# First loads in smaller pieces behind a warm-up product, and two pieces of VectorE work moved off the round changes, in a two-layer mixing and feed-forward kernel

## The chip, the core and the metric

The kernel runs on one core of one Trainium2 chip, in float32. The metric is the device time of one execution in microseconds, as the median of several runs. One execution is also taken by the hardware profiler; all instruction times below come from that one.

## The reference, cut to what matters

The input x has 32 samples of 128 channels by 2048 columns. The first layer computes `x + F(M(x))`. M mixes the 128 channels of each sample with a kernel of its own, a sum of eight matrices weighted by a softmax of the sample's condition. F multiplies the 2048 columns by a 2048 x 2048 matrix W and adds a low-rank update:

```
out = jnp.einsum('bsd,od->bso', x, W) + bias
xa  = jnp.einsum('bsd,erd->ebsr', x, A)
w   = coeffs * scales
upd = jnp.einsum('ebsr,eor,e->bso', xa, Bf, w)
return out + upd
```

The second layer is a grouped convolution with nine taps along the columns, then sixteen heads of a feed-forward block (128 to 512 to 128, with a Gelu) over permuted columns.

## The kernel before, in words

Mixing by channel and multiplying by columns commute, so the kernel first multiplies x by the whole weight and mixes afterwards.

**The weight.** W plus the low-rank update (256 ranks, in two halves c of 128) is made in 16 blocks of 512 x 2048 numbers. `w_make` (L150) makes one: four times two products of a piece of A with a piece of B^T (L156), and a VectorE add of W to each result (L160). It stores the block with a DMA on GpSimd's queue (L162). The ranks have factors `wsc`, coeffs times scales; before, they are multiplied into B^T by `low_scale` on VectorE (L140). A and B^T are loaded in four quarters of 512 columns each by `load_low`, each half c by a DMA of its own, all on SP's queue. Four blocks are made before the first step. The rest are made two to a step in the first round.

**The big product.** It is done by Strassen-like recursion: seven outer products P1, P2, P6, P7, P5, P3, P4, called rounds, each with eight steps g (four samples each), 56 steps in all. A step (`multiply`, L256) is itself seven inner products of 4 x 2 TensorE records (L272), 24.03 us in all. Their results lie in three PSUM banks: P1, P6, P7, P4 go to px, P2 to pz, P5 and P3 to py. In time they run P1 (px), P2 (pz), P6 (px), P5 (py), P7 (px), P3 (py), P4 (px). VectorE adds each result to SBUF (L265) before the next product into the same bank may start; in the first round ScalarE copies those that are new (L267). `inner_weights` (L175) makes three or four differences of weight blocks once per round: on VectorE before the first step, on GpSimd later, during step g=7 of a round or just before it (L179 to L185, about 4.5 us each). `x_combine` (L213) makes the four sums of x for a step on GpSimd, `outer_weights` (L303) combines weight blocks for the coming round there.

**Order.** The order of every engine's instructions is the order of the Python program (a manual schedule); each queue runs in that order. Between the inner products, `between(j)` hands small pieces of other work to the engines. One piece is `mixed_kernel` (L337): eight VectorE instructions on 128 x 128 numbers (L345, L347) that make the mixed kernel of one sample, two after each of the first four products. Kernel b = (round - 1) * 7 + g falls to step g of each round after the first, for g = 0 to 6, until 32 are made; after 16 of them GpSimd stores the buffer (L349). The generator `small` (L578) is advanced once at the end of each step: the condition's layers, products of the weight's column sums with ones (L672), then the matrices of the convolution (tw): three loads at the end of step 6 (L680 to L682), four VectorE instructions (L684 to L687) and a store on SP's queue (L688) at the end of step 7, the last of round P1.

**Buffers.** A pool of 24 SBUF buffers of 8 KB per partition holds nearly everything; a load waits on SP's queue until its buffer is free. From the last round on, the mixing, convolution and feed-forward work (L381, L436, L540, L551) are interleaved with it and follow it.

Of the kernel before, what the change touches and what calls it, by code (L numbers as in the profile page):

```python
# [11 lines left out]
ALU = mybir.AluOpType  # L12
# [4 lines left out]
P = 128  # L17
B = 32
L = 2048
QW = 512  # L20
KEXP = 8
# [4 lines left out]
NQ = QW // 2  # L26
# [4 lines left out]
NG = B // GB  # L31
# [11 lines left out]
def adaln_ffn_kernel(  # L43
# [16 lines left out]
    A: bass.AP,  # L60
    BfT: bass.AP,
    coeffs: bass.AP,
    scales: bass.AP,
    toep: bass.AP,
    cwT: bass.AP,
    ffw: bass.AP,
# [3 lines left out]
    nc = tc.nc  # L70
# [8 lines left out]
    def slot(name, shape=(P, L)):  # L79
        return big.tile(list(shape), FP, name=name, tag="s")  # L80


    def bank():
        return banks.pop(0)

    def done(*ps):
        banks.extend(ps)
# [29 lines left out]
    wsc = const.tile([P, 2], FP, name="wsc", tag="wsc")  # L117
    cs = const.tile([P, 4], FP, name="cs", tag="cs")


    nc.sync.dma_start(cs[:, 0:2], coeffs)
    nc.sync.dma_start(cs[:, 2:4], scales)
    nc.vector.tensor_tensor(wsc, cs[:, 0:2], cs[:, 2:4], ALU.mult)
    a_sb = [slot(f"a_sb{c}") for c in range(2)]
    bf_sb = [slot(f"bf_sb{c}") for c in range(2)]

    def load_low(k, o):

        for c in range(2):
            if o is not None:  # L130
                cols = bass.ts(o, QW)
                nc.sync.dma_start(bf_sb[c][:, cols], BfT[c, :, cols])
        for c in range(2):
            if k is not None:
                nc.sync.dma_start(a_sb[c][:, bass.ts(k, QW)], A[c, :, bass.ts(k, QW)])

    def low_scale(o):
        for c in range(2):
            cols = bf_sb[c][:, bass.ts(o, QW)]
            nc.vector.tensor_scalar(cols, cols, wsc[:, c : c + 1], None, ALU.mult)  # L140

    wsum = slot("wsum", (P, NPH, QW))
    seen = set()

    def w_load(kh, oh, ki, oi):
        t = slot(f"w_{kh}{oh}{ki}{oi}", (P, 4, QW))
        nc.sync.dma_start(t.rearrange("p k o -> p (k o)"), WT[kh, oh, ki, oi])
        return t

    def w_make(t, kh, oh, ki, oi):  # L150
        o = 2 * oh + oi
        for kc in range(4):
            pw = bank()
            i0 = kh * 1024 + ki * 512 + kc * P
            for c in range(2):
                nc.tensor.matmul(  # L156
                    pw, lhsT=a_sb[c][:, i0 : i0 + P], rhs=bf_sb[c][:, bass.ts(o, QW)],
                    start=(c == 0), stop=(c == 1),
                )
            nc.vector.tensor_tensor(t[:, kc], pw, t[:, kc], ALU.add)  # L160
            done(pw)
        nc.gpsimd.dma_start(wb_d[kh, oh, ki, oi], t.rearrange("p k o -> p (k o)"))  # L162

    def row_sums(t, oh, oi):
        o = 2 * oh + oi
        ks = t.rearrange("p k o -> p o k")
        if o in seen:
            part = agp.tile([P, QW], FP, name=f"part_{len(seen)}", tag="sn", bufs=2)
            nc.vector.tensor_reduce(part, ks, AX.X, ALU.add)
            nc.vector.tensor_tensor(wsum[:, o], wsum[:, o], part, ALU.add)  # L170
        else:
            nc.vector.tensor_reduce(wsum[:, o], ks, AX.X, ALU.add)
        seen.add(o)
# [15 lines left out]
    def x_load(g, tp, kh):  # L189
        t = slot(f"xt_{g}{tp}{kh}", (P, 2, 2, QW))  # L190
        nc.sync.dma_start(t.rearrange("p k s c -> p (k s c)"), xT[g, tp, kh])
        return t
# [385 lines left out]
    def small():  # L578
# [3 lines left out]
        def load(name, src, rows, cols, eng=nc.scalar):  # L582
            t = sm[0:rows, used[0] : used[0] + cols]
            used[0] += cols
            if src is not None:
                eng.dma_start(t, src)
            return t
# [17 lines left out]
        ones = load("ones", None, P, P)  # L605
# [63 lines left out]
        wbc = slot("wbc", (P, NPH, QW))  # L669
        for o in range(NPH):  # L670
            p5 = bank()
            nc.tensor.matmul(p5, lhsT=ones, rhs=wsum[:, o], start=True, stop=True)  # L672
            nc.scalar.copy(wbc[:, o], p5)
            done(p5)
        nc.sync.dma_start(w1_d, wbc.rearrange("p f n -> p (f n)"))
# [5 lines left out]
        nc.sync.dma_start(tw[:, 2], toep[:, 0])  # L681
        nc.sync.dma_start(tw[:, 3], toep[:, 2])  # L682
        yield
        nc.vector.tensor_tensor(tw[:, 1], tw[:, 2], tw[:, 3], ALU.add)  # L684
        nc.vector.tensor_scalar(tw[:, 1], tw[:, 1], 0.5, None, ALU.mult)  # L685
        nc.vector.scalar_tensor_tensor(tw[:, 0], t1, 0.5, tw[:, 1], ALU.mult, ALU.add)  # L686
        nc.vector.scalar_tensor_tensor(tw[:, 1], t1, -0.5, tw[:, 1], ALU.mult, ALU.add)  # L687
        nc.sync.dma_start(tw_d, tw.rearrange("p k r c -> p (k r c)"))  # L688
        yield
# [6 lines left out]
        for kh, oh in ((0, 0), (0, 1), (1, 1), (1, 0)) for ki in range(2) for oi in range(2)  # L696
    ]
    first = {}
    load_low(0, 0)
    wt = {k: w_load(*k) for k in blocks[0:1]}  # L700
    low_scale(0)
    load_low(None, 1)
    low_scale(1)
    wt[blocks[1]] = w_load(*blocks[1])
    load_low(1, None)
    xs = {0: [x_load(0, 0, 0)]}
    for k in blocks[2:4]:
        wt[k] = w_load(*k)

    def make(k):  # L710
        t = wt.pop(k)
        w_make(t, *k)
        made.append(k)
        if len(made) > 4:
            row_sums(t, k[1], k[3])
        return t

    steps = [(r, g) for r in ROUNDS for g in range(NG)]
    xs[0] += [x_load(0, 1, 0), x_load(0, 1, 1)]
    load_low(2, 2)  # L720
    load_low(3, 3)
    lhs = {}
    for n, k in enumerate(blocks[0:4]):
        first[k[2:]] = make(k)
        if n == 1:
            lhs[0] = x_combine(*steps[0], xs.pop(0))
    low_scale(2)
    low_scale(3)
    rhs = inner_weights("P1", first, nc.vector)
    unsummed = [(0, 0), (1, 0), (1, 1)]  # L730
    olds = {}
# [1 line left out]
    nxt, waiting, ts = {}, {}, {}  # L733
# [8 lines left out]
    for i, (r, g) in enumerate(steps):  # L742
        ri = i // NG
        last_round = ri + 1 == len(ROUNDS)
        if i + 1 < len(steps):
            if i + 1 not in xs:
                xs[i + 1] = x_loads(*steps[i + 1])
            if not last_round:
                lhs[i + 1] = x_combine(*steps[i + 1], xs.pop(i + 1))
                x_outer()  # L750
        if i + 2 < len(steps) and ri > 0 and not last_round:
            xs[i + 2] = x_loads(*steps[i + 2])
        if i == 0:
            olds_load(0)
        if i + 1 < len(steps) and not last_round:
            olds_load(i + 1)
        if g == NG - 1 and 0 < ri < len(ROUNDS) - 1:
            nxt = inner_weights(ROUNDS[ri + 1], nxt)

        if ri == 0:  # L760
            for k in blocks[4 + 2 * g : 6 + 2 * g]:
                t = make(k)
                if "late" in first:
                    b12 = first.pop("late")
                    row_sums(b12, 0, 1)
                    nc.vector.tensor_tensor(b12, first[1, 1], b12, ALU.subtract)
                if k[:2] == (1, 0):
                    nxt[k[2:]] = t
        elif ri + 1 < len(ROUNDS):
            for k, combine in waiting.items():  # L770
                nxt[k] = combine()
            waiting = {}
            if 2 <= g < 6:
                k = ((g - 2) // 2, (g - 2) % 2)
                waiting[k] = outer_weights(ROUNDS[ri + 1], *k)

        if last_round and g == 0:
            late_loads()
        k0 = 3 * (g - NG)
        if last_round:  # L780
            stage(k0, stage_first)

        def between(j):
            b = (ri - 1) * (NG - 1) + g
            if ri > 0 and g < NG - 1 and b < B and j < KEXP // 2:
                mixed_kernel(b, (2 * j, 2 * j + 1))
            if ri == 0 and j == 2:
                for k in blocks[6 + 2 * g : 8 + 2 * g]:
                    wt[k] = w_load(*k)
            if ri == 0 and j == 4 and unsummed:  # L790
                ki, oi = unsummed.pop(0)
                row_sums(first[ki, oi], 0, oi)
            if last_round:
                if j == 3 and i + 1 < len(steps):
                    lhs[i + 1] = x_combine(*steps[i + 1], xs.pop(i + 1))
                    olds_load(i + 1)
                if j in (2, 4):
                    stage(k0 + j // 2, stage_first)
                stage(k0 + j // 2, stage_third if j % 2 else stage_second)

        multiply(r, g, lhs.pop(i), rhs, olds.pop(i), between)
        next(chain, None)
        if last_round and g >= 6:
            pair(g - 6)
        if last_round and g == 7:
            gather_two(0)
        if g == NG - 1 and ri + 1 < len(ROUNDS):
            rhs = nxt if ri > 0 else inner_weights(ROUNDS[ri + 1], nxt)
            nxt = {}

    before = None
    for k, (g, h) in enumerate(heads):
# [5 lines left out]
        t = ts.pop(k)  # L818
# [70 lines left out]
```

## Time and profile before

| | |
|---|---|
| median of 3 runs | 2712.27 us (2712.09 to 2712.54) |
| profiled execution, its own time | 2712.6 us |
| its span, first to last instruction | 2710.8 us |
| TensorE busy | 2680.0 us in 6232 records |
| VectorE, GpSimd, ScalarE busy | 1266.6, 1087.6, 438.0 us |
| mean granted TensorE clock | 0.997 |
| first product (L156) starts | 7.35 us |
| first step's first product (L272) starts | 52.73 us |
| DMA moved | 608.03 MB, mean 224 GB/s |

How to read it: a float32 product of 128 x 128 by 128 x 512 shows as two records, each with a weight load before it. A line of a timeline or of a group gives the engine, the line of the program, the operation, what is written and read, shapes and a count; square brackets give the idle time before it and what ended it. The waits name the engine and the line that was waited for. A line can be that of a helper, so that all products of `multiply` have L272. Start and duration of a TensorE row are modelled, since its records overlap.

### The profile page before, as it was taken

The numbers are of one execution on the slowest core, as the hardware profiler recorded it, in microseconds if no ns is written. First come the engines' busy times: TensorE is split into PE (matmuls) and PEld (weight loads), VectorE is DVE, ScalarE is ACT, GpSimd is POOL, SyncE is SP. The second block draws the span as 40 slices with busy tenths as digits, with TensorE's granted clock in tenths as the row PEclk, the third lists the DMA queues.
The fourth block names the chain that finished last, engine by engine and source line by source line (L and its number), as shares of the span: only waits on it lengthen the run. The fifth ranks groups of instructions, "written<-read, shape, count | busy, mean of one in ns | idle before, by whom it ended". The sixth has DMA issues, their size and how long they took to land.

```text
span 2710.8 us, 18770 instructions
## 1 busy us (share of the span) xinstructions
PE 2680.0 (99%) x6232; PEld 1183.9 (44%) x6232; DVE 1266.6 (47%) x1934; ACT 438.0 (16%) x811; POOL 1087.6 (40%) x633
## 2 busy tenths in 40 slices
PE   8999999999999999999999999999999999999998
PEld 3444344444444444444444444444444444444443
DVE  5554333433445456432265555555555545555400
ACT  0000000000000000000000133333333333333332
POOL 3544546523655323647222233333334333333322
PEclk9999999999999999999999999999999999999999
DMA  8875547445465466575657888777777677777532
GB/s 339 344 295 224 205 192 306 152 186 205 158 258 233 176 240 253 215 285 195 216 191 234 260 286 247 228 233 230 212 222 231 214 219 231 227 226 239 168 116 85
DMA packets 184256, 608.03 MB, mean 224 GB/s; under 512 B 18016, under 2 KB 87904, under 8 KB 139744
## 3 DMA queue, kind: packets, MB, share of 16 engines
q1 hardware_dynamic: 148384, 465.36, 49.0%
q0 software_dynamic: 34144, 140.53, 15.1%
q10 hardware_dynamic: 1632, 0.96, 0.1%
q8 instruction: 50, 0.82, 0.1%
q14 instruction: 46, 0.38, 0.0%
HBM read 363.50 MB, written 209.72 MB: 211 GB/s over the span
## 4 chain that ended last, share of the span: by engine, by line
PE 96%; DVE 3%; issue 0%; DMA 0%; SPq 0%; POOLq 0%; DVEq 0%
PE bank L272 47%; PE bank L540 16%; PE bank L551 16%; PE bank L436 8%; PE bank L156 4%; PE bank L381 4%; DVE ags L347 2%; DVE u L265 0%; DVE tw L686 0%; DVE tw L685 0%; DMA a_sb<-in_A 0%; PE bank L672 0%; DVE p L265 0%; DMA out<-t,orow 0%; POOLq L884 0%
## 5 line engine op out<-in xcount | busy, mean ns | idle before, releaser
L540 PE MATMUL bank<-t,ws 128*128 128x512 f32 x1024 | 460.2, 592 | 0.0
L551 PE MATMUL bank<-gl,ws 128*128 128x512 f32 x1024 | 460.2, 592 | 0.0
L557 POOL DMA_INDIRECT out<-t,orow x128 | 154.9, 1210 | 662.7 <-DVE t L555 401.7
L543 ACT ACTIVATE gl<-bank 128x512 f32<-128x512 f32 x512 | 303.6, 597 | 689.1 <-PE bank L540 590.0
L272 PE MATMUL bank<-P_t,s_P 128*128 128x512 f32 x896 | 396.1, 595 | 6.2 <-DVE p L265 6.2
L265 DVE TENSOR_TENSOR u<-bank,u 128x512 f32<-128x512 f32 x280 | 187.8, 687 | 428.7 <-PE bank L272 419.6
L555 DVE TENSOR_TENSOR t<-bank,t 128x512 f32<-128x512 f32 x128 | 88.4, 691 | 557.8 <-PE bank L551 557.8
L540 PEld LDWEIGHTS bank<-t,ws 128*128 128x128 f32 x1024 | 194.6, 190 | 244.9 <-issue 241.3
L551 PEld LDWEIGHTS bank<-gl,ws 128*128 128x128 f32 x1024 | 194.6, 190 | 244.9 <-issue 236.8
L272 PE MATMUL bank<-wo_P,s_P 128*128 128x512 f32 x640 | 283.6, 593 | 3.3 <-DVE u L265 3.0
L272 PEld LDWEIGHTS bank<-P_t,s_P 128*128 128x128 f32 x896 | 170.9, 191 | 222.1 <-issue 221.4
L448 ACT ACTIVATE sn<-bank,ctxb 128x256 f32<-128x256 f32 x128 | 53.7, 471 | 1130.3 <-PE bank L436 1129.0
L436 PE MATMUL bank<-v,tw_l 128*128 128x512 f32 x512 | 235.6, 592 | 0.0
L371 POOL TENSOR_TENSOR x<-x,fb 128x2048 f32<-128x2048 f32 x32 | 144.7, 4522 | 168.7 <-DVE x L368 108.2
L272 PEld LDWEIGHTS bank<-wo_P,s_P 128*128 128x128 f32 x640 | 120.9, 190 | 159.0 <-issue 148.5
L265 DVE TENSOR_TENSOR p<-bank,p 128x512 f32<-128x512 f32 x112 | 77.3, 691 | 239.9 <-PE bank L272 239.7
L347 DVE SCALAR_TENSOR_TENSOR ags<-mix,att_bc,ags 128x128 f32<-128x128 f32 x224 | 185.9, 830 | 4.5
L272 PE MATMUL bank<-wo_P,xt 128*128 128x512 f32 x384 | 169.2, 592 | 0.0
L223 POOL TENSOR_TENSOR s_P<-xt 128x512 f32<-128x512 f32 x40 | 51.0, 1276 | 271.4 <-DMA xt<-in_xT 218.3
L523 POOL DMA_INDIRECT t<-hx_d,row x128 | 137.8, 1077 | 37.1 <-issue 33.6
L436 PEld LDWEIGHTS bank<-v,tw_l 128*128 128x128 f32 x512 | 97.2, 190 | 122.8 <-issue 121.5
L272 PE MATMUL bank<-P_t,xt 128*128 128x512 f32 x320 | 145.6, 598 | 3.1 <-DVE p L265 3.1
(114 smaller groups left out, 2493.5 us busy)
## 6 DMA issues: line engine op xcount, KB each, us to landing
xt<-in_xT SPq DMA_DIRECT2D x64, 1024.0 KB, 8.6
u<-u_d SPq DMA_DIRECT2D x40, 1024.0 KB, 10.6
wo_P<-wb_d SPq DMA_DIRECT2D x36, 1024.0 KB, 12.5
u<-c_d SPq DMA_DIRECT2D x64, 512.0 KB, 6.9
x<-in_x SPq DMA_DIRECT2D x32, 1024.0 KB, 8.8
xg<-x SPq DMA_DIRECT2D x256, 128.0 KB, 7.4
hx_d<-x1t SPq DMA_DIRECT2D x32, 1024.0 KB, 4.9
hx_d<-ht SPq DMA_DIRECT2D x32, 1024.0 KB, 7.3
```

The costliest lines, as they stand in the source:

```text
L156: nc.tensor.matmul(pw, lhsT=a_sb[c][:, i0 : i0 + P], rhs=bf_sb[c][:, bass.ts(o, QW)], start=(c == 0), stop=(c == 1),)
L265: nc.vector.tensor_tensor(to, ps, to, ALU.add)
L272: nc.tensor.matmul(ps, lhsT=lhs[k][:, bass.ts(kc, P)], rhs=rhs[k][:, kc], start=first and kc == 0, stop=last and kc == 3, skip_group_check ...
L347: nc.vector.scalar_tensor_tensor(ag, mix[:, k], att, ag, ALU.mult, ALU.add)
L371: nc.gpsimd.tensor_tensor(xt, xt, late["fb"], ALU.add)
L381: nc.tensor.matmul(pm, lhsT=ag, rhs=u[:, f], start=True, stop=True)
L436: nc.tensor.matmul(ps, lhsT=late["tw"][:, k, r], rhs=v[k], start=first, stop=last, skip_group_check=True,)
L523: nc.gpsimd.indirect_dma_start(out=t.rearrange("p k t -> p (k t)"), out_offset=None, in_=hx_d[g].rearrange("l k t -> l (k t)"), in_offset= ...
L540: nc.tensor.matmul(pu, lhsT=w[:, m * P : (m + 1) * P], rhs=t[:, 0], start=True, stop=True)
L543: nc.scalar.activation(gl[:, m], pu, AF.Gelu)
L551: nc.tensor.matmul(pd, lhsT=w[:, (MC + m) * P : (MC + m + 1) * P], rhs=gl[:, m], start=(m == 0), stop=(m == MC - 1),)
L557: nc.gpsimd.indirect_dma_start(out=out, out_offset=bass.IndirectOffsetOnAxis(ap=orow[:, g, h : h + 1], axis=0), in_=t[:, 1], in_offset=None,)
```

## The change

It has five parts.

1. *First loads.* A and B^T are kept as two tiles of 1024 columns that hold both rank halves; the host lays them out so that one DMA brings both halves. The two small vectors come in one DMA. The first load of A is 128 columns, the first two of B^T 256 columns each; then come the remaining 384 of A's first quarter, and quarters.
2. *Scaling.* The factors are multiplied into A, not into B^T: A's quarters are scaled after their loads, the second quarter after the first block is made, the third and fourth after the fourth block.
3. *Warm-up.* TensorE first does two products of a zeroed tile that nothing reads. The first product of the first block is done in two halves of 256 columns.
4. *Conv matrices.* L684 to L687 are spread: the generator waits one step more, then L684 and L685 run at the end of step 8 (P2, g=0), L686 after step 9 and L687 with the store after step 10.
5. *Mixed kernels.* Kernel b = (round - 1) * 6 + g falls to g = 0 to 5; the last two are made in the last round, P4, at g = 0 and 1. The products with ones (L672) are done in two halves of 256 columns.

```diff
-    nc.sync.dma_start(cs[:, 0:2], coeffs)
-    nc.sync.dma_start(cs[:, 2:4], scales)
-    nc.vector.tensor_tensor(wsc, cs[:, 0:2], cs[:, 2:4], ALU.mult)
-    a_sb = [slot(f"a_sb{c}") for c in range(2)]
-    bf_sb = [slot(f"bf_sb{c}") for c in range(2)]
-    def load_low(k, o):
-        for c in range(2):
-            if o is not None:
-                cols = bass.ts(o, QW)
-                nc.sync.dma_start(bf_sb[c][:, cols], BfT[c, :, cols])
-        for c in range(2):
-            if k is not None:
-                nc.sync.dma_start(a_sb[c][:, bass.ts(k, QW)], A[c, :, bass.ts(k, QW)])
-    def low_scale(o):
-        for c in range(2):
-            cols = bf_sb[c][:, bass.ts(o, QW)]
+    a_sb = [slot(f"a_sb{h}", (P, 2, L // 2)) for h in range(2)]
+    bf_sb = [slot(f"bf_sb{h}", (P, 2, L // 2)) for h in range(2)]
+    def low(ts, c, i0, n):
+        h, i0 = divmod(i0, L // 2)
+        return ts[h][:, c, i0 : i0 + n]
+    def low_load(ts, src, i0, n):
+        h, j0 = divmod(i0, L // 2)
+        nc.sync.dma_start(ts[h][:, :, j0 : j0 + n], src[:, :, i0 : i0 + n])
+    def a_scale(i0, n):
+        for c in range(2):
+            cols = low(a_sb, c, i0, n)
             nc.vector.tensor_scalar(cols, cols, wsc[:, c : c + 1], None, ALU.mult)
+    def warm_up():
+        t = slot("warm", (P, QW))
+        nc.vector.memset(t, 0.0)
+        pw = bank()
+        for _ in range(2):
+            nc.tensor.matmul(pw, lhsT=t[:, 0:P], rhs=t, start=True, stop=True)
+        done(pw)
...
-            for c in range(2):
-                nc.tensor.matmul(
-                    pw, lhsT=a_sb[c][:, i0 : i0 + P], rhs=bf_sb[c][:, bass.ts(o, QW)],
-                    start=(c == 0), stop=(c == 1),
-                )
+            n = QW // 2 if i0 == 0 and o == 0 else QW
+            for o0 in range(0, QW, n):
+                for c in range(2):
+                    nc.tensor.matmul(
+                        pw[:, o0 : o0 + n], lhsT=low(a_sb, c, i0, P),
+                        rhs=low(bf_sb, c, o * QW + o0, n), start=(c == 0), stop=(c == 1),
+                    )
...
-            nc.tensor.matmul(p5, lhsT=ones, rhs=wsum[:, o], start=True, stop=True)
+            for half in (slice(0, NQ), slice(NQ, QW)):
+                nc.tensor.matmul(
+                    p5[:, half], lhsT=ones, rhs=wsum[:, o, half], start=True, stop=True
+                )
...
         yield
+        yield
         nc.vector.tensor_tensor(tw[:, 1], tw[:, 2], tw[:, 3], ALU.add)
         nc.vector.tensor_scalar(tw[:, 1], tw[:, 1], 0.5, None, ALU.mult)
+        yield
         nc.vector.scalar_tensor_tensor(tw[:, 0], t1, 0.5, tw[:, 1], ALU.mult, ALU.add)
+        yield
         nc.vector.scalar_tensor_tensor(tw[:, 1], t1, -0.5, tw[:, 1], ALU.mult, ALU.add)
         nc.sync.dma_start(tw_d, tw.rearrange("p k r c -> p (k r c)"))
...
-    load_low(0, 0)
+    warm_up()
+    nc.sync.dma_start(cs, coeffs)
+    low_load(a_sb, A, 0, P)
+    low_load(bf_sb, BfT, 0, QW // 2)
+    low_load(bf_sb, BfT, QW // 2, QW // 2)
+    nc.vector.tensor_tensor(wsc, cs[:, 0:2], cs[:, 2:4], ALU.mult)
+    a_scale(0, P)
+    low_load(a_sb, A, P, QW - P)
+    a_scale(P, QW - P)
     wt = {k: w_load(*k) for k in blocks[0:1]}
-    low_scale(0)
-    load_low(None, 1)
-    low_scale(1)
+    low_load(bf_sb, BfT, QW, QW)
     wt[blocks[1]] = w_load(*blocks[1])
-    load_low(1, None)
+    low_load(a_sb, A, QW, QW)
...
-    load_low(2, 2)
-    load_low(3, 3)
+    for i0 in (1024, 1536):
+        low_load(bf_sb, BfT, i0, QW)
+        low_load(a_sb, A, i0, QW)
     lhs = {}
     for n, k in enumerate(blocks[0:4]):
         first[k[2:]] = make(k)
+        if n == 0:
+            a_scale(QW, QW)
         if n == 1:
             lhs[0] = x_combine(*steps[0], xs.pop(0))
-    low_scale(2)
-    low_scale(3)
+    for i0 in (1024, 1536):
+        a_scale(i0, QW)
     rhs = inner_weights("P1", first, nc.vector)
...
-            b = (ri - 1) * (NG - 1) + g
-            if ri > 0 and g < NG - 1 and b < B and j < KEXP // 2:
+            b = (ri - 1) * (NG - 2) + g
+            if ri > 0 and g < NG - 2 and b < B and j < KEXP // 2:
                 mixed_kernel(b, (2 * j, 2 * j + 1))
```

## The prediction

> **What bounds the kernel now.** I read the page first, then TensorE's waits, then the timelines of the few places where TensorE stands still. The page says that TensorE is the bound: 2680.0 us of the span of 2710.8.
>
> ```profile
> PE 2680.0 (99%) x6232; PEld 1183.9 (44%) x6232; DVE 1266.6 (47%) x1934; ACT 438.0 (16%) x811; POOL 1087.6 (40%) x633
> ...
> PE 96%; DVE 3%; issue 0%; DMA 0%; SPq 0%; POOLq 0%; DVEq 0%
> ```
>
> The change takes no product away, so it can only gain what TensorE waits, and what it loses by running slowly. All its waits over the whole span:
>
> ```profile
> PE bank L272 <- DVE p L265: 9.7, 3, 6.2
> PE bank L156 <- DMA a_sb<-in_A: 7.4, 1, 7.4
> PE bank L272 <- DVE u L265: 3.0, 7, 0.5
> PE bank L156 <- DVE bf_sb L140: 1.2, 1, 1.2
> ```
>
> They sum to 21.3 us (columns: total, times, longest). Window by window: 7.4 and 1.2 lie in the first 40 us, 6.24 and 3.12 in the second round (P2), 0.3 in the third, 2.1 in the fourth, 0.8 in the sixth. After about 1173 us there is none.
>
> The longest, at the change from round P1 to P2, in the timelines of TensorE, VectorE and GpSimd (start, duration, instruction):
>
> ```profile
> 332.88 9.13 PE L272 MATMUL bank<-P_t,s_P 128*128 128x512 f32 x16 [6.24 <-DVE p L265]
> ...
> 317.71 4.62 DVE L685 TENSOR_SCALAR tw<-tw 128x512 f32<-128x512 f32 x1
> 322.36 4.88 DVE L686 SCALAR_TENSOR_TENSOR tw<-t,tw 128x512 f32<-128x512 f32 x1
> 327.27 4.87 DVE L687 SCALAR_TENSOR_TENSOR tw<-t,tw 128x512 f32<-128x512 f32 x1
> 332.06 0.68 DVE L265 TENSOR_TENSOR p<-bank,p 128x512 f32<-128x512 f32 x1
> ...
> 317.19 4.85 POOL L180 TENSOR_TENSOR P_t<-w,P_t 128x2048 f32<-128x2048 f32 x1
> 322.00 4.69 POOL L184 TENSOR_TENSOR w<-w,w 128x2048 f32<-128x2048 f32 x1
> 326.65 4.94 POOL L185 TENSOR_TENSOR P_t<-w,P_t 128x2048 f32<-128x2048 f32 x1
> ```
>
> The conv matrices (tw) run on VectorE step by step with the round's weight differences on GpSimd; the add that frees px is queued behind them. After the wait 16 records take 9.13 us, where 16 elsewhere take 7.03: another 2.10 us.
>
> The second place is step g=6 of round P2, where two mixed-kernel instructions meet two weight differences:
>
> ```profile
> 486.87 8.68 DVE L347 SCALAR_TENSOR_TENSOR ags<-mix,att_bc,ags 128x128 f32<-128x128 f32 x2
> ...
> 496.20 5.40 PE L272 MATMUL bank<-P_t,xt 128*128 128x512 f32 x8 [3.12 <-DVE p L265]
> ```
>
> 8 records take 5.40 instead of 3.60: 1.80 us more. Last the start:
>
> ```profile
> 7.35 30.36 PE L156 MATMUL bank<-bf_sb,a_sb 128*128 128x512 f32 x64 [7.35 <-DMA a_sb<-in_A]
> 38.89 14.00 PE L156 MATMUL bank<-bf_sb,a_sb 128*128 128x512 f32 x32 [1.18 <-DVE bf_sb L140]
> ...
> 40.27 0.49 DVE L140 TENSOR_SCALAR bf_sb<-bf_sb,wsc 128x512 f32<-128x512 f32 x1 [0.62 <-DMA bf_sb<-in_BfT]
> 40.67 2.28 DVE L179 TENSOR_TENSOR P_t<-w,w 128x2048 f32<-128x2048 f32 x1
> ...
> 47.53 2.48 DVE L160 TENSOR_TENSOR w<-bank,w 128x512 f32<-128x512 f32 x4
> ```
>
> A record costs 0.4292 us where TensorE runs freely (24.03 us for 56). 64 would take 27.5; they took 30.2 (30.36 less the 0.16 by which a record overlaps the next), so the slow beginning costs 2.7. And the DMA engines are full here:
>
> ```profile
> 15.00:45.00 30.00, 28.82 (x67) 12.46 (x66) 15.57 (x20) 0.00 (x0) 7.47 (x8) 1.00 1.02 414
> ```
>
> (the last two columns: DMA share 1.02, 414 GB/s).
>
> **What the Trainium skill says.** "SBUF — State Buffer", section "SBUF: two separate sides": VectorE and GpSimd share a port pair that one of them holds for a whole instruction. The trace agrees: L347 has a median of 0.352 us and a maximum of 4.637, beside GpSimd operations of 4.5. "TensorE: Matmul & The Clock Gate", "What's actually happening": the array runs at half clock until it has been busy for a window of about 3.4 us, and falls back after an idle one. Half speed agrees (weight loads 0.85 us apart until 12 us, 0.43 after); but here a wait of only 3.12 cooled it, and one of 1.18 did not (14.00 us for 32 records, 13.98 for the same 32 later). "DMA: Bandwidth & Descriptors", "Queues, rings and completion order": an engine takes turns between its queues. From 28 to 34 us loads moved 1.43 MB and GpSimd's stores 1.05 MB, which agrees.
>
> **The change part by part.**
>
> *Conv matrices.* The three blocked instructions leave the round change; L684 and L685 run at the end of step g=0 of P2, L686 at the end of g=1 and L687 at the end of g=2. Removed: 6.24 + 2.10 = 8.34 us. Their new cost: L140, L685's form, takes 0.49; L686 I put at 0.6, a quarter of L368's 2.34 with four times its columns; if GpSimd holds the pair, 5.2 at worst. Each follows the last add of a step; the next add falls due one product (3.43 us) later and must be done before the product after that starts: 6.87 us for two adds (0.69 each) and the instruction between them, 0.49 + 0.68 likely, 5.9 at worst. So 0, at worst 0.4 each. The tw store now waits on SP's queue behind one such instruction, at most 5 us, not 11.3; the loads behind it (xt, p) land 7 to 10.5 us after issue and are due about 20 later. What is late next: the P6 product needs L180, done at 322.04, and comes at 326.65; nothing is.
>
> *Mixed kernels.* Step g=6 of four rounds is cleared: 3.12 + 1.80, and 0.3 in P6: 5.2 us. Kernels 24 to 29 land in P3, two of them at g=4 and g=5 where there was none, and 30 and 31 in P4 at g=0 and g=1. P3's own g=1 and g=2 paid 0.39 and 0.43 where L220 (4.51) met the pair. At g=4 L220 (1214.93) hits the third pair likewise: 0.4. At g=5 it starts at 1239.99, after that pair, and holds the fourth until 1244.5, before the next add is due at 1245.29: 0. P4 g=0: GpSimd idle. g=1: L371 (4.51 from 1334.2) delays one pair, and four records of L381 follow: 0 to 0.4. I take 0.5 for all; at worst a double hit as at 486.87, 4.9. L349 waits for the last kernel ahead of P4's combinations on GpSimd, by some 4 us, which are wanted 13 later: 0.
>
> *Halved products with ones.* 8 records become 16 of half the columns; a weight load (0.190) fits into half a record (0.215): 0.1, at worst 8 x 0.19 = 1.5.
>
> *The start.* The first needed bytes fall from 1 MB to 0.39 MB. The first bf piece landed 3.6 us after its issue; now it is issued near 1.6, so the product starts at 5.0 (4.3 to 5.8), not 7.35. The warm-up product (four records at 0.85 from about 1.2, after a memset that I put at 0.5 like L140) runs in idle time and takes most of the 2.7 away. The rest of A[0:512] lands at 7.4 (now 7.9 for as many bytes, issued 0.5 earlier), two scales of 0.36 make it 8.1, and 60 records end at 33.9 instead of 37.7. **But the DMA stream does not get shorter.** The same 11.5 MB come before the last piece of A in the same order, and GpSimd's stores start 3.3 us sooner, at 1 MB per 6.86 us: 0.5 MB more ahead of it, 1.2 us at 414 GB/s. The piece of B for the fifth block landed at 35.0 and now does near 35.5; so TensorE waits 1.6 there and ends the fifth and sixth blocks (32 records, 13.7) at 49.2. VectorE now scales A, not B: it waits for A[1536:2048], which landed at 42.3 and now does at 42.3 - 0.5 + 1.2 = 43.0; before it waited only for B, until 40.26. Behind that wait on VectorE stand two scales (0.9), the three weight differences and the first add of the fifth block (40.67 to 48.2, 7.5), and the first product of step 0 needs that add's bank: 43.0 + 8.4 = 51.4. It started at 52.73: a gain of 1.3, not the 4.8 that the start promises. Bounds: a landing from 40 to 45, that is a gain of 4.8 (TensorE's own limit, no wait for B) down to a loss of 0.7.
>
> **Sum:** 8.34 + 5.2 + 1.3 - 0.5 - 0.1 = 14.2 off the profiled 2712.6 (span 2710.8 and 1.8 around it). The median of the runs is 2712.27, 0.3 lower: 2698.0.
>
> **Rivals.** (1) *The start keeps its gain* (0.20): the last A piece lands by 40, since fewer, larger loads and earlier issue keep the queue fuller; 3.5 more, 2694.5. For it: most loads are issued many us earlier. Against: the engines are already at 1.02. (2) *New waits* (0.22): the wait of some 2.2 us ahead of step 0 cools the clock as 3.12 did (2.0), or a new place in P3 or P4 takes a double hit (4.9): 2700 to 2704. (3) *The change doesn't do what it says* (0.04): the tw instructions meet GpSimd's pairs L325 and L327, which sit at 392 to 401 in g=2, and wait as before: 8.3 given back, and perhaps a second such wait, 2706 to 2710. (4) *Slower* (0.04): the second group of mixed kernels holds one of 24 buffers for six more steps, P3 g=4 to P4 g=1. If loads on SP's queue then wait for a release, TensorE stalls once the wait passes 24.03 - 10.6 = 13.4 us per step; at 20 us it is 6.6 x 6 = 40, so 2738, and it decides from 13.4 + 14.2/6 = 15.8 on. Against: the same buffer is held through P5, the fullest round, and SP's longest wait for a buffer there is 0.9.
>
> **How the numbers follow.** Likeliest 0.50, 2696 to 2700. The range 2693 to 2703 leaves out (3), (4) and the ends of (1) and (2). A measurement of this kernel tells 0.2%, 5.4 us, from no change. Faster: 0.50 + 0.20 + 0.22 = 0.92; within: 0.04; slower: 0.04.
>
> **What would show it.** Right: no wait near 319 to 333 nor in g=6 of P2; L685 to L687 under 2 us; first L156 near 5; VectorE waiting for a_sb near 43 and TensorE for VectorE ahead of step 0. Wrong: step 0 starting before 50 (rival 1), L272 records at half speed near 52 (rival 2), SP waits for buffers of many us after 1200 (rival 4).

## The result, and the profile after

| | before | after |
|---|---|---|
| median of the runs | 2711.88 us (6, 2710.47 to 2712.54) | 2701.08 us (6, 2698.99 to 2704.26) |
| ratio, 95% interval | | 0.9962 (0.9949 to 0.9975) |
| profiled execution, span | 2712.6, 2710.8 us | 2702.9, 2701.1 us |
| first product of step 0 | 52.73 us | 55.10 us |
| first product of step 8 (P2, g=0) | 319.61 us | 322.00 us |
| first product of round P6 | 525.47 us | 516.36 us |

The kernel became 0.38% faster by the ratio, 10.8 us by the medians. In a second set of runs of the same kernel, beside three others on one chip, it was 2702.99 us against 2711.11: 0.9973 (0.9964 to 0.9982), spread from 2699.18 to 2707.93. The three last rows of the table say where to look: the start **lost** 2.4 us, round P2 gained 11.5, and the rest of the kernel gained another 0.6.

TensorE's waits over the whole span of the changed kernel (total, times, longest; L279 is the old L272, L163 the old L156, L135 the scaling, L143 the warm-up):

```profile
PE bank L163 <- DVE a_sb L135: 3.4, 1, 3.4
PE bank L279 <- DVE u L272: 3.2, 8, 0.5
PE bank L163 <- DMA bf_sb<-in_BfT: 2.5, 2, 2.2
PE bank L279 <- DVE p L272: 1.9, 1, 1.9
PE bank L143 <- DVE warm L140: 1.5, 1, 1.5
```

The waits for p have shrunk from 9.7 us to 1.9. The start has four waits where it had two. TensorE's timeline there:

```profile
1.46 3.78 PE L143 MATMUL bank<-warm 128*128 128x512 f32 x4 [1.46 <-DVE warm L140]
5.54 2.43 PE L163 MATMUL bank<-bf_sb,a_sb 128*128 128x256 f32 x8 [0.29 <-DMA bf_sb<-in_BfT]
11.37 26.02 PE L163 MATMUL bank<-bf_sb,a_sb 128*128 128x512 f32 x60 [3.40 <-DVE a_sb L135]
39.59 15.67 PE L163 MATMUL bank<-bf_sb,a_sb 128*128 128x512 f32 x32 [2.21 <-DMA bf_sb<-in_BfT]
```

The first product does start 1.8 us earlier (5.54, not 7.35), and the 60 full records that follow run at full speed: 26.02 us, where 60 x 0.4292 is 25.8. But the remaining piece of A comes at 10.9, and B's third quarter at 39.5. After the wait for it, 2.21 us, the array ran slowly for a while (it cooled: the granted clock was 0.65 from 40 to 42 us and 0.50 from 42 to 44): 32 records took 15.67 us, 1.7 more than the 13.97 at full speed. VectorE's timeline shows how near it was to being the bound as well:

```profile
40.84 0.88 DVE L135 TENSOR_SCALAR a_sb<-a_sb,wsc 128x512 f32<-128x512 f32 x2 [2.72 <-DMA a_sb<-in_A]
45.63 0.88 DVE L135 TENSOR_SCALAR a_sb<-a_sb,wsc 128x512 f32<-128x512 f32 x2 [3.91 <-DMA a_sb<-in_A]
46.43 2.28 DVE L186 TENSOR_TENSOR P_t<-w,w 128x2048 f32<-128x2048 f32 x1
...
53.29 2.48 DVE L167 TENSOR_TENSOR w<-bank,w 128x512 f32<-128x512 f32 x4
```

The first add ends near 54.0, TensorE reaches step 0 at 55.1, so in this execution B's landing and the slow records behind it set the start of step 0, and VectorE's path lay 1.1 us behind. At the round change the conv matrices are gone, and the first mixed kernel stands in their place, in the way of the same four weight differences (VectorE, then GpSimd, then TensorE):

```profile
326.25 3.62 DVE L352 TENSOR_SCALAR ags<-mix,att_bc 128x128 f32<-128x128 f32 x1
329.90 4.49 DVE L354 SCALAR_TENSOR_TENSOR ags<-mix,att_bc,ags 128x128 f32<-128x128 f32 x1
334.31 0.68 DVE L272 TENSOR_TENSOR p<-bank,p 128x512 f32<-128x512 f32 x1
...
325.26 4.52 POOL L191 TENSOR_TENSOR w<-w,w 128x2048 f32<-128x2048 f32 x1
329.72 4.52 POOL L192 TENSOR_TENSOR P_t<-w,P_t 128x2048 f32<-128x2048 f32 x1
...
337.75 7.11 PE L279 MATMUL bank<-w,s_P 128*128 128x512 f32 x16 [1.85 <-DVE p L272]
```

Both instructions of the pair are held to the ends of L191 and L192 (329.78 and 334.24), as the sharing of a port pair in the Trainium skill's page "SBUF — State Buffer", section "SBUF: two separate sides", has it. The spread conv matrices themselves cost no wait: L696, the old L685, took 0.43 us, L698 and L700 took 0.68 and 0.81.

### The profile page after: what moved, and what is told of

It is laid out like the page before. It is cut to its first block, busy times and chain, and to the rows that moved or that the text cites. A ratio compares the mean times of both kernels' runs of the same rounds, so it can differ in the third digit from the quotient of the medians.

```text
span 2701.1 us, 18790 instructions
## 1 busy us (share of the span) xinstructions
PE 2679.1 (99%) x6248; PEld 1186.0 (44%) x6248; DVE 1260.9 (47%) x1937; ACT 438.0 (16%) x811; POOL 1085.7 (40%) x633
## 3 DMA queue, kind: packets, MB, share of 16 engines
q1 hardware_dynamic: 148656, 465.35, 49.4%
## 4 chain that ended last, share of the span: by engine, by line
PE 95%; DVE 3%; DMA 1%; SPq 0%; issue 0%; POOLq 0%
PE bank L279 47%; PE bank L547 16%; PE bank L558 16%; PE bank L443 8%; PE bank L388 4%; PE bank L163 3%; DVE ags L354 2%; DMA bf_sb<-in_BfT 1%; DVE u L272 0%; DVE ags L352 0%; PE bank L680 0%; DMA out<-t,orow 0%; SPq L130 0%; DVE p L272 0%; POOLq L907 0%
## 5 line engine op out<-in xcount | busy, mean ns | idle before, releaser
L279 PE MATMUL bank<-P_t,s_P 128*128 128x512 f32 x896 | 394.0, 592 | 0.0
L272 DVE TENSOR_TENSOR u<-bank,u 128x512 f32<-128x512 f32 x280 | 187.9, 688 | 418.9 <-PE bank L279 410.1
L279 PE MATMUL bank<-wo_P,s_P 128*128 128x512 f32 x640 | 283.6, 593 | 3.2 <-DVE u L272 3.2
L279 PEld LDWEIGHTS bank<-P_t,s_P 128*128 128x128 f32 x896 | 170.2, 190 | 214.3 <-issue 213.8
L272 DVE TENSOR_TENSOR p<-bank,p 128x512 f32<-128x512 f32 x112 | 77.3, 690 | 247.8 <-PE bank L279 247.7
L279 PEld LDWEIGHTS bank<-wo_P,s_P 128*128 128x128 f32 x640 | 120.9, 190 | 158.9 <-issue 148.3
L279 PE MATMUL bank<-wo_P,xt 128*128 128x512 f32 x384 | 169.2, 592 | 0.0
L279 PE MATMUL bank<-P_t,xt 128*128 128x512 f32 x320 | 143.8, 592 | 0.0
```

The source lines that it names most:

```text
L272: nc.vector.tensor_tensor(to, ps, to, ALU.add)
L279: nc.tensor.matmul(ps, lhsT=lhs[k][:, bass.ts(kc, P)], rhs=rhs[k][:, kc], start=first and kc == 0, stop=last and kc == 3, skip_group_check ...
```

## The experiments

Every run computes the whole result. The ratio is to the kernel before in the same set of runs; there are three sets of four.

| run | median us (range) | before | ratio, 95% interval |
|---|---|---|---|
| x1_old_start | 2699.29 (2698.33 to 2699.63) | 2710.68 | 0.9956 (0.9942 to 0.9969) |
| x2_start_only | 2716.12 (2710.44 to 2719.45) | 2710.68 | 1.0018 (1.0011 to 1.0024) |
| x3_conv_only | 2703.53 (2702.52 to 2704.43) | 2710.68 | 0.9973 (0.9963 to 0.9983) |
| x4_first_mixed_late | 2704.01 (2698.78 to 2705.13) | 2710.68 | 0.9972 (0.9961 to 0.9983) |
| x0_changed_again | 2702.99 (2699.18 to 2707.93) | 2711.11 | 0.9973 (0.9964 to 0.9982) |
| x5_scale_later | 2699.94 (2697.97 to 2701.89) | 2711.11 | 0.9962 (0.9949 to 0.9976) |
| x6_b_before_x | 2703.90 (2698.23 to 2705.85) | 2711.11 | 0.9969 (0.9957 to 0.9980) |
| x7_whole_first | 2700.03 (2698.28 to 2701.04) | 2711.11 | 0.9960 (0.9947 to 0.9974) |
| x8_no_warm | 2701.91 (2697.34 to 2706.45) | 2711.09 | 0.9970 (0.9959 to 0.9981) |
| x9_three_mends | 2696.96 (2695.45 to 2698.85) | 2711.09 | 0.9947 (0.9934 to 0.9961) |
| x10_old_start_warm | 2698.98 (2697.61 to 2699.27) | 2711.09 | 0.9951 (0.9938 to 0.9965) |
| x11_old_start_warm_late | 2697.41 (2696.84 to 2698.04) | 2711.09 | 0.9947 (0.9934 to 0.9961) |

**The change taken apart.** x1_old_start is the kernel before with the conv matrices and the mixed kernels as changed:

```diff
-            b = (ri - 1) * (NG - 1) + g
-            if ri > 0 and g < NG - 1 and b < B and j < KEXP // 2:
+            b = (ri - 1) * (NG - 2) + g
+            if ri > 0 and g < NG - 2 and b < B and j < KEXP // 2:
...
+        yield
         nc.vector.tensor_tensor(tw[:, 1], tw[:, 2], tw[:, 3], ALU.add)
         nc.vector.tensor_scalar(tw[:, 1], tw[:, 1], 0.5, None, ALU.mult)
+        yield
         nc.vector.scalar_tensor_tensor(tw[:, 0], t1, 0.5, tw[:, 1], ALU.mult, ALU.add)
+        yield
```

> The kernel before with only the conv matrices spread and the mixed kernels moved; loads, scaling, start and ones products as before. Theory (the new start costs): step 0 starts at 52.7 again, the wait of 1.9 at the first step of P2 stays, time 2698.7, 2.4 below the changed kernel's 2701.1. Rival (the new start is neutral, its later step 0 is hidden or made good later): 2701, as the changed kernel. My prediction's sum without its start: 2699.6.

Measured 2699.29, 11.4 below before, and with a spread of 1.3 us. x2_start_only is the complement: the changed kernel with these lines put back.

> The changed kernel with the conv matrices and the mixed kernels put back to their old places; the new start alone. Theory (the new start costs): step 0 starts near 55.1 instead of 52.7 and the time is 2714.3, 2.4 over before. Rival (it is neutral or gains, as predicted): 2710.6 to 2711.9. The wait at the first step of P2 should be 6.2 again in both.

Measured 2716.12: 5.4 over before by the medians, 1.8 per mille by the ratio, twice what the one profile had shown. The new start does not gain, it costs. How much is known only roughly: 11.4 less 5.4 is 6.0, while the changed kernel gained 10.8 and 8.1 in its two sets. The profiled execution of x2, the longest of 21, shows the wait that the prediction had put ahead of step 0, and one more behind it (TensorE's waits):

```profile
PE bank L279 <- DVE p L272: 10.6, 3, 7.4
PE bank L163 <- DMA bf_sb<-in_BfT: 4.2, 2, 3.5
PE bank L279 <- DVE u L272: 2.8, 7, 0.5
PE bank L279 <- DVE w L785: 2.6, 1, 2.6
PE bank L279 <- DVE w L167: 1.6, 1, 1.6
```

L167 is the first add; L785 is the late weight difference of step 0 (L766 of the kernel before). x3_conv_only has the three added `yield`s alone.

> The kernel before with only the conv matrices spread over three steps. Theory (the first mixed kernel steps into the place of the conv matrices, because GpSimd's weight differences still run there): the wait of 6.2 becomes 1.9 with no slow records behind it, 6.4 gained, 2705.5; the wait of 3.1 in step g=6 of P2 stays. Rival (the prediction's: nothing else is late there): 8.3 gained, 2703.6.

Measured 2703.53, 7.15 below before, between the two expectations, whose 6.4 and 8.3 lie both in the interval. The profile decides: in place of the wait of 6.24 stands one of 0.70, again behind L345 and L347 held by L184 and L185 (2.45 and 4.49 us). So the mechanism of the first theory is there; its size, 1.85 in the changed kernel, depends on when the difference starts. The wait in g=6 was 3.5. The mixed kernels are worth what x1 has over x3: 4.2.

**The first mixed kernel.** x4_first_mixed_late, the changed kernel with:

```diff
-            if ri > 0 and g < NG - 2 and b < B and j < KEXP // 2:
-                mixed_kernel(b, (2 * j, 2 * j + 1))
+            q = j - 2 if ri == 1 and g == 0 else j
+            if ri > 0 and g < NG - 2 and b < B and 0 <= q < KEXP // 2:
+                mixed_kernel(b, (2 * q, 2 * q + 1))
```

> The changed kernel, but in the first step of P2 the four pairs of mixed-kernel instructions come after the third to sixth product, not the first to fourth. Theory (the wait of 1.9 there is the first pair meeting two weight differences): the wait goes, below 0.4 is left, 1.9 less: 2699.2. Rival (the add is late for another reason, such as the old partial sums' load): the wait stays and 2701.1.

The wait is gone: TensorE runs from 324.27 through the whole of P2 without one. Yet the median is 2704.01, not 2699.2. The gain is covered by the start: the profiled execution waits 1.03 for the first add and 2.60 for the late difference. On this start a mend of 1.9 us can't be read from the time; x11 below tries it on the old start.

**Why the start loses, and why it spreads.**

> The changed kernel itself, on the chip of the three runs beside it, for the spread of its time. In the runs so far kernels with the new start spread over 5 to 9 us, those with the old one over 1 to 3. Theory (in the first step the difference of weights on VectorE races GpSimd's sums for the shared port and loses in part of the executions): 2699 to 2705, in two heaps some 4 us apart. Rival (the spread is that of the chip): as narrow as the kernel before, 2 to 3 us.

Measured from 2699.18 to 2707.93, while before spread from 2709.13 to 2713.39. The eleven runs are rather spread than in two heaps; that part of the expectation failed. The profiled execution, a short one (2699.38), starts step 0 at 52.02 and waits for B only once, 0.8 us for its first piece. It differs from the first profile in the landings: B's third quarter at 37.0, not 39.5, and A's last piece at 43.6, not 45.6. x5_scale_later moves the scaling that waits for that piece:

```diff
-    for i0 in (1024, 1536):
-        a_scale(i0, QW)
     rhs = inner_weights("P1", first, nc.vector)
...
+            if g == 1:
+                for i0 in (1024, 1536):
+                    a_scale(i0, QW)
```

> The changed kernel with the scaling of A's third and fourth quarter moved behind the weight making of the second step, so that VectorE doesn't wait for their loads ahead of the first weight differences. Theory (that wait makes VectorE late, and its difference of weights meets GpSimd's sums): no wait for L167 or for the difference in step 0, VectorE's differences start near 38 instead of 46, narrow spread, 2699 to 2700; step 0 still starts near 55, since B's piece lands at 39.5. Rival (my prediction: the wait on VectorE alone sets step 0's start): step 0 starts near 51 and the time is 2697.

VectorE's differences start at 35.58, no wait on L167 is left, the median is 2699.94, 3 below the changed kernel beside it (the intervals of the two ratios overlap), and the spread is 4 instead of 9. So the wait for A matters; it does not set step 0 alone, since TensorE then waits 3.2 us for B (step 0 at 51.96, not near 55, as B landed 1.4 us earlier here). x6_b_before_x takes B's wait away and leaves A's:

```diff
+    for i0 in (1024, 1536):
+        low_load(bf_sb, BfT, i0, QW)
     xs[0] += [x_load(0, 1, 0), x_load(0, 1, 1)]
     for i0 in (1024, 1536):
-        low_load(bf_sb, BfT, i0, QW)
         low_load(a_sb, A, i0, QW)
```

> The changed kernel with the loads of B's third and fourth quarter put ahead of two x loads that are needed later. Theory (both B's late landing and VectorE's wait for A bind, one 1.3 us behind the other): the wait of 2.2 for B goes, but step 0 starts no earlier than 54, since the first add waits for A; 2699 to 2704, as wide as before. Rival (B's landing alone binds): step 0 starts near 51.2, 3.9 less: 2697.

The four lines of its profile (TensorE, then VectorE) are the prediction's mechanism in its pure form:

```profile
6.02 43.39 PE L163 MATMUL bank<-bf_sb,a_sb 128*128 128x256 f32 x100 [0.77 <-DMA bf_sb<-in_BfT]
54.94 10.04 PE L279 MATMUL bank<-w,xt 128*128 128x512 f32 x16 [5.53 <-DVE w L167]
...
46.55 0.88 DVE L135 TENSOR_SCALAR a_sb<-a_sb,wsc 128x512 f32<-128x512 f32 x2 [0.42 <-DMA a_sb<-in_A]
...
54.20 2.48 DVE L167 TENSOR_TENSOR w<-bank,w 128x512 f32<-128x512 f32 x4
```

TensorE is through with six blocks at 49.4 and then waits 5.53 for the first add, behind the differences, behind A. After that wait 16 records take 10.04 us, 3.0 more than 7.03. The time, 2703.9, is that of the changed kernel: one wait took the place of the other. x7_whole_first asks whether small pieces make the later ones land late:

```diff
-    low_load(a_sb, A, 0, P)
-    low_load(bf_sb, BfT, 0, QW // 2)
-    low_load(bf_sb, BfT, QW // 2, QW // 2)
+    low_load(a_sb, A, 0, QW)
+    low_load(bf_sb, BfT, 0, QW)
     nc.vector.tensor_tensor(wsc, cs[:, 0:2], cs[:, 2:4], ALU.mult)
-    a_scale(0, P)
-    low_load(a_sb, A, P, QW - P)
-    a_scale(P, QW - P)
+    a_scale(0, QW)
```

> The changed kernel with the first quarters of A and of B^T each in one load of 2 KB pieces, not in two loads each of 0.5 to 1.5 KB pieces. Theory (small pieces make the stream slow at first, 257 and 217 GB/s from 4 to 8 us against 292 and 357 before): the first quarter of A is scaled by 8.9 instead of 11.3, all later loads land 1 us or more earlier, B's third quarter by 38.5; 1 us less. Rival (more bytes in flight make everything land late, the piece size doesn't matter): A's first quarter still after 10.5, time unchanged.

From 4 to 10 us the DMA engines moved 349 GB/s here, 281 in the changed kernel and 336 before (DMA share 0.98, 0.92, 0.98). The first quarter of A is scaled from 5.89 on, not 10.89; B's first quarter lands at 9.7, so that the first product starts 4.2 us later than in the changed kernel. Even so TensorE then waits for nothing up to step 0, which starts at 53.21, and the median is 3 below the changed kernel beside it, again with intervals that overlap. So small pieces do slow the first microseconds (270 to 309 GB/s in all profiles with them, 332 to 349 in those without). That they make the late pieces late is not shown: A's last piece is scaled from 43.54 on here and from 43.63 on in x0, and in x8 below, with the same small pieces and the slowest beginning of all (270 GB/s from 4 to 10 us), from 42.26 on.

**The warm-up.** x8_no_warm leaves the call of `warm_up()` out of the changed kernel.

> The changed kernel without the warm-up product. Theory (the start is set by when loads land, so that early TensorE speed is given back at the wait for B): the first four blocks end 1 to 2.5 us later, the wait for B shrinks by as much, step 0 starts when it did; time as the changed kernel, 2699 to 2705. Rival (the warm-up is worth what the slow records cost before): 2.7 slower, 2704 to 2706.

2701.91, no different from the changed kernel by the intervals of the two sets; with a spread of 9 us in both, 2.7 us could hardly be told from nothing. Its profiled execution is one of the two shortest (2697.34): the 8 half records take 3.75 us instead of 2.43, and none of that is seen at step 0, which starts at 50.66. Nor did the warm-up bring full speed everywhere: in x9 below the 100 records behind it take 43.84 us, where 8 halves and 92 full ones at full speed would take 41.4 (an estimate from 0.4292 a record). x10_old_start_warm puts the warm-up ahead of the old loads, with x1's other edits:

```diff
-    nc.vector.tensor_tensor(wsc, cs[:, 0:2], cs[:, 2:4], ALU.mult)
...
+    warm_up()
+    nc.vector.tensor_tensor(wsc, cs[:, 0:2], cs[:, 2:4], ALU.mult)
     load_low(0, 0)
```

> The kernel before with the conv matrices spread, the mixed kernels moved and the warm-up product, but with its own loads and scaling of B. Theory (the old loads land early enough, 35.0 for B's third quarter, and VectorE waits only until 40.3, so the slow records are a real cost here): the first 64 records take 27.6 instead of 29 to 30, step 0 starts 1.5 to 2.7 earlier, 2697. Rival (here too the loads or VectorE set step 0): 2699.3, as without the warm-up.

The rival holds: 2698.98 against 2699.29. The zeros end at 5.2, A lands at 7.99, the granted clock is 0.50 from 10 to 12 us, and the 64 records take 29.40, between the 29.22 (x1) and 30.36 (before) without it.

**Versions that beat both.** x9_three_mends joins the edits of x4, x5 and x6.

> The changed kernel with three mends together: A's late quarters scaled behind the second step's weight making, B's late quarters loaded ahead of two x loads, the first mixed kernel two products later. Theory (step 0 was bound twice, by B's landing and by VectorE's wait for A, so that each mend alone gave little): no wait for B or for L167 ahead of step 0, which starts near 50 to 50.5; the wait at P2's first step goes; 2696.5, 4 to 5 below the changed kernel. Rival (something third is late there, such as the fifth block of W, which landed at 48.2 in the run with the scaling moved, or the weight difference that meets GpSimd): step 0 starts near 52 or waits inside, 2699.

2696.96, 6.0 below the changed kernel in the neighbouring set (another chip; before took 2711.1 in both). Its TensorE waits, all of them:

```profile
PE bank L279 <- DVE u L272: 3.3, 8, 0.5
PE bank L143 <- DVE warm L140: 1.5, 1, 1.5
PE bank L163 <- DMA bf_sb<-in_BfT: 0.7, 1, 0.7
```

100 records of the first six blocks run in one piece (43.84 us from 5.92), and step 0 starts at 49.60: 5.5 earlier than in the changed kernel's first profile, 2.4 earlier than in x0. A's and B's landing had bound it both: with either mend alone TensorE met the other wait (3.22 for B in x5, 5.53 for the add behind A in x6). x11_old_start_warm_late is x10 with x4's edit.

> The kernel before it with, besides, the first mixed kernel two products later in the first step of P2: my candidate for the best version. Theory: 0.6 to 1.9 less than without that, 2695.5 to 2696.5, with a spread of 2 like the kernel before. Rival (the wait there was gone already): 2697 as well.

2697.41, 1.6 below x10, with a spread of 1.2. The wait of 0.7 that x10 has in P2 is gone; the rest may be noise, since the runs of the two overlap (x10 from 2697.61, x11 to 2698.04). With the old loads the kernel is as fast as with the mended new ones; both are 0.53% faster than before.

## Why the prediction was right, and where it was wrong

The prediction was 2698.0 us in a range of 2693 to 2703; the two sets of runs gave 2701.1 and 2703.0 (the second median right at the range's end). The stretch called likeliest, 2696 to 2700, was missed; both medians lie in rival 2's 2700 to 2704. The gains at the two VectorE places were forecast for the right reason and nearly at their size. The start was forecast with the wrong sign, and that the total stayed in the range all the same is in part luck: the range had room for it. By its steps:

- **Conv matrices: size off.** 8.34 was forecast; 7.15 was measured for them alone. The 6.24 of wait and the 2.10 of slow records did go. The term that failed is "What is late next ...; nothing is": it looked at TensorE's inputs, not at what stands next on VectorE's queue. The first pair of mixed kernel 0 stood there and took 0.70 (x3) to 1.85 us (the changed kernel) back, until x4 and x11 moved it. So the sign named for "right", no wait near 319 to 333, held in letter only: one of 1.85 us ends at 337.75.
- **Mixed kernels: right.** Forecast 5.2 less 0.5; x1 against x3 says 4.2. The wait of P2's g=6 and its slow records are gone. In P3 four waits of 1.6 in all stand for two of 0.8: 0.8 more, not 0.4. Nothing was found in P4.
- **Halved products with ones: right.** The chain has 3.45 us for 16 halves, 3.43 for the 8 before.
- **Buffers (rival 4) and conv instructions that stall elsewhere (rival 3): did not come.**
- **The start: the waits right, the landings and the sign wrong.** Forecast a gain of 1.3; measured a loss of 2.4 in the profile, of 5.4 by x2's median, and of 1.8 and 3.7 by the changed kernel's two medians against x1's. That loads, not TensorE, would set step 0, with VectorE's new wait for A in the middle, is what x5, x6 and x9 show. But the landings were set too early: the rest of A's first quarter 10.9 (forecast 7.4), B's third quarter 39.5 (35.5), A's last piece 45.6 (43.0). The reason given for the delay, stores that start 3.3 us sooner, was not the one in the first profile: the first store went out at 17.83 us, before at 18.16. (In x4 and x2 it went out at 17.06 and 16.06, so there it may have had a part.) The step that failed is "The same 11.5 MB come before the last piece of A in the same order": it lets every load land when the bytes up to it in the queue have been moved. What SP's queue had moved (packets, MB, share) when the rest of A's first quarter had landed, before by 7.9 us and in the changed kernel by 10.8, and when A's last piece had, by 42.3 and by 45.6:

```profile
q1 hardware_dynamic: 920, 1.51, 61.2%
q1 hardware_dynamic: 1456, 2.23, 68.4%
...
q1 hardware_dynamic: 3694, 12.31, 76.2%
q1 hardware_dynamic: 4038, 12.78, 73.6%
```

In the queue's order 1.05 MB lie up to the first of these pieces. The changed kernel had moved as much by 7.4 us, the very time of the forecast, but the piece landed 3.4 us later. Up to A's last piece lie 11.5 MB; these were moved by about 40.7 us, before by about 40.1; the piece landed 4.9 us after that, before 2.2. So the slower stream of small pieces (281 against 336 GB/s from 4 to 10 us) makes some 0.6 of the 3.3 us; the rest passes while loads from further back are moved ahead of it, 1.25 MB by the end, before 0.8. A likely reason is that most loads of A and B are now twice as large, so that more bytes are under way behind a piece; no run varies that by itself, so it is not shown.
- **Cooling (rival 2): came,** in the changed kernel after the wait for B at 39.6 us (1.7 us), and ahead of step 0, where it was put, in x6 (3.0).

What stays open: why the same loads land A's last piece at 42.3 (x8), 43.6 (x0) or 45.6 in different executions. Where VectorE does not wait for it (x5, x9), or the first pieces are larger (x7, x10, x11), the spread is 1.2 to 4 us instead of 8.7 (of five runs each, against eleven); the late difference, which took 2.3 to 7.1 us depending on who of VectorE and GpSimd had the port pair first, adds to it (2.60 of TensorE's wait in x4).

## What to carry to other kernels

While the DMA engines are full, an earlier first product can be worth nothing by itself, as here: ask what lands last ahead of the next stage, and who waits for it in queue order. Don't take a load as landed when the bytes up to it have been moved: look in the trace how many bytes of later loads get ahead of it. When a stall is taken off an in-order queue, the next instruction on that same queue inherits its place; look there before writing that nothing is late next. Two bounds that lie a microsecond apart need both mends in one run: here one alone measured as nothing (x6), and the other as a gain within the scatter (x5).

## What was not expected of the hardware

- Waits of 2.21 us (the changed kernel), 2.74 (x10) and 2.84 (x0) cooled the array, while ones of 2.47 (x4), 3.22 (x5), 3.40 (the changed kernel) and 3.48 (x2) did not (13.97 us for 32 records, 26.02 for 60). The clock fell only after the wait: that of 2.21 us was over at 39.59, and the granted clock was 0.65 from 40 to 42 us, 0.50 from 42 to 44 and 0.99 from 44 to 46. The Trainium skill's page "TensorE: Matmul & The Clock Gate", "What's actually happening", calls the window free-running and has the array fall back after an idle one of about 3.4 us. A wait of 2.21 us holds no whole window, so the measurement differs from the page here; that a shorter wait cools and a longer one doesn't says that more than the wait's length counts, and no run here tests what.
- A VectorE instruction that needs the port pair can be held by a GpSimd instruction that starts after it. In x4 the late difference began at 63.32 us, while GpSimd issued a DMA; the GpSimd sum of 4.52 us that began at 63.75 went first, and the difference took 7.11 us. In x9 it began at 57.62, 0.07 ahead of the sum, and took 2.29, and the sum took 6.62.
- SP's issue of one load of 512 KB took 5.20 us itself in the changed kernel, where 0.55 is usual; the same is seen in x2 (7.04) and x4 (5.86), but not in x7 (1.21). Why is not shown.
